# Projection's steps four ahead of the attention's, column sums in the projection's spare bank, and another order of ScalarE's work at a group's turn

## The chip, the cores and the metric

The kernel runs on one core of a Trainium2 chip. The metric is the device time of one execution in microseconds (us); it is given as the median of three runs. Beside it stands one execution taken with the hardware profiler, from which all rows of the profile come. PE is TensorE's matmul row, PEld its weight loads, DVE VectorE, ACT ScalarE, POOL GpSimd and SP SyncE; a small q behind a name means the queue that issues transfers.

## The reference

Four images x of 64 x 64 pixels and 256 channels go through one self-attention layer in float32. Cut to what matters:

```python
q = einsum('bwhc,cd->bwhd', x, Wq) + bq        # d = 128
k = einsum('bwhc,cd->bwhd', x, Wk) + bk
v = einsum('bwhc,cd->bwhd', x, Wv) + bv        # 256 channels
pq, pk, pv = (t.reshape(B, -1, N) for t in (q, k, v))   # N = 4096
energy = einsum('bcn,bcm->bnm', pq, pk)
attention = softmax(energy, axis=-1)
out = einsum('bcm,bnm->bcn', pv, attention)
return gamma * out.reshape(x.shape) + x
```

## The kernel before, in words

**Forms.** A float32 operand is split into a high form h (ScalarE, a scaled copy that is rounded to the matmul's type), a rest l and a combined form d (VectorE, two instructions). A product then is three matmuls instead of one, and each product's accumulator is corrected between two of them.

**Attention.** The loop `for n in range(B * STEPS)` runs 512 steps: 4 images (b) x 8 groups (g) of 512 columns n x 16 steps (t) of 256 rows m. What a step n issues belongs to several steps, since the work is pipelined: the energies of step n + 2 (LOOK = 2), the forms of n + 1, and the attention's product of n. In order: `cross(n + 2)` (two matmuls, L298, into the two banks of `ps_e`, and two scalings by ScalarE, L299), `attend(n, 0)` (six matmuls L355 into the banks a0 and b0), `energy(n + 2)` (four matmuls L313 and two Exp by ScalarE, L316, into x), `upper(n + 2)` (ScalarE's h of it, L322), `halves(n + 1)` (VectorE: L331 adds x to the running column sum s, L336 makes l, L338 makes d), `attend(n, 1)` (six matmuls L355 into a1 and b1). Each engine takes its instructions in the order in which the program issues them; the schedule is written by hand and nothing reorders it. So a step is 18 matmuls of 512 columns on TensorE, and on ScalarE two L299, two L316 and one L322.

**The turn of a group.** a0, a1, b0 and b1 accumulate over the 16 steps of a group. At t = 15, `sum_forms` splits the column sums s into zf (ScalarE L378, VectorE L379, issued ahead of `halves`), and `emptied(n, 0)` copies a0 and b0 into the buffer o (two ScalarE instructions, L369). At t = 0 of the next group, right after `cross`, `emptied(n - 1, 1)` copies a1 and b1, and `sums(n - 1)` multiplies zf by ones (two matmuls, L384) into bank b1 and lets ScalarE copy one row of the result, L385. Then `finish`, a generator that moves on by one piece at the end of each step, takes reciprocals by way of two small DRAM buffers (zd, rd), scales o, adds x by a GpSimd transfer, and stores the result.

**Projection.** Image 0 is projected ahead of the loop. The images 1 to 3 are projected inside it, one image ahead: each of the 16 blocks i of an image takes 8 of the loop's steps, and `step(n, engine)` issues what belongs to r = n mod 8. TensorE has four transposes at r = 0 (L191), the first part of q and k at r = 3 (four matmuls of 256 columns, L222), their second part at r = 4 (eight), the first of v at r = 5 and its second at r = 6. ScalarE has x's h at r = 1 (L202), the h of q and k at 5 (L248), v's bias at 6 (L240) and v's h at 7 (L153). VectorE has one or two instructions at r = 0, 1, 2, 3 (L233, which seeds the second part), 5, 6 and 7. The projection's accumulators rotate over the two banks of the pool `ps_p`. The last image's 128 steps have no projection beside them. Since 16 is twice 8, r = t mod 8: the turn's two steps, t = 15 and t = 0, have r = 7 and r = 0.

**Transfers.** GpSimd's queue stores the forms of q, k and v to DRAM (kf, qd and vf, issued by `store()`, one step after VectorE has made them), loads k for step n + 5 in each step (L285, three buffers), q once a group at t = 6, and in the last group of an image v of the next image, one piece a step from t = 3 on. SyncE's queue loads x for the projection (L183), and carries zd, rd and the output.

Of the kernel before, what the change touches and what calls it, by code (L numbers as in the profile page):

```python
# [9 lines left out]
F32 = mybir.dt.float32  # L10
# [5 lines left out]
PSUM = bass.MemoryType.PSUM  # L16
# [4 lines left out]
def kernel(  # L21
# [37 lines left out]
    B, W, H, C = x.shape  # L59
    P = 128  # L60
# [21 lines left out]
    NB = 512  # L82
    NJ = NB // P
    NG = N // NB
    NU = NM // 2
    STEPS = NG * NU
    LOOK = 2
# [13 lines left out]
    with ExitStack() as fast:  # L101
        fast.enter_context(tc.manual_schedule())
        pool = lambda name, bufs, **kw: fast.enter_context(
            tc.tile_pool(name=name, bufs=bufs, **kw)
        )
# [3 lines left out]
        kpool = pool("kpool", 3)  # L109
        dram = pool("dram", 2, space=DRAM)  # L110
        ps_e = pool("ps_e", 2, space=PSUM)
        ps_p = pool("ps_p", 2, space=PSUM)
        ps_o = pool("ps_o", 1, space=PSUM)


# [27 lines left out]
        qd, kf, vf, units, loads, now = {}, {}, {}, {}, {}, {}  # L143
# [20 lines left out]
        def image(b):  # L164
            for g in range(NG):
                qd[b, g] = dram.tile([P, NJ, 3, P], F32R, tag=f"qd{g}", name=f"qd_{b}_{g}")
            for t in range(NU):
                kf[b, t] = dram.tile([P, 2, 3, P], F32R, tag=f"kf{t}", name=f"kf_{b}_{t}")
                vf[b, t] = dram.tile([P, 3, 2, C], F32R, tag=f"vf{t}", name=f"vf_{b}_{t}")

        def bank(name, shape):
            pool, tag = next(now["banks"])
            return pool.tile(shape, F32, tag=tag, name=name)

        def load_x(b, i):
            if i >= NI:
                return
            if b == 0:
                t = xs4[:, i % 4]
            else:  # L180
                t = work.tile([P, 2, XB], F32, tag="xin", name=f"x_{b}_{i}", bufs=1)
            if b or i:
                nc.sync.dma_start(t, xv[b, i])  # L183
            loads["x", b, i] = t
# [107 lines left out]
        def cross(n):  # L292

            if n >= B * STEPS:
                return
            for i in range(2):
                e = units["e", n, i] = ps_e.tile([P, NB], F32, tag="e", name=f"e_{n}_{i}")
                nc.tensor.matmul(e, *forms(n, i, 2), start=True, stop=False, skip_group_check=True)  # L298
                nc.scalar.mul(e, e, -REST)  # L299
# [18 lines left out]
        def upper(n):  # L318
            if n >= B * STEPS:
                return  # L320
            h = ppool.tile([P, 2, NB], F32R, tag="h", name=f"h_{n}", bufs=3)
            nc.scalar.activation(h, units[n], AF.Identity, scale=UPPER)  # L322
            units[n] = units[n], h
# [40 lines left out]
        def emptied(n, j):  # L364

            if j == 0:
                now["o"] = work.tile([P, 2, 2, NB], F32, tag="o", name=f"o_{n // NU}", bufs=1)
            for c, scale in enumerate((gam2, gam1)):
                nc.scalar.activation(  # L369
                    now["o"][:, c, j, :], now["ab"[c], j], AF.Identity, scale=scale  # L370
                )

        def sum_forms(n):

            s = now["total"] = now["sum"]
            f = work.tile([P, 2, NB], F32R, tag="r", name=f"zf_{n // NU}", bufs=1)
            h, l = now["z"] = f[:, 0, :], f[:, 1, :]
            nc.scalar.activation(h, s[:, 0, :], AF.Identity, scale=UPPER)  # L378
            nc.vector.tensor_tensor(l, s[:, 0, :], h.bitcast(F32), ALU.subtract)  # L379

        def sums(n):
            zp = ps_o.tile([P, NB], F32, tag="b1", name=f"z_{n // NU}")
            for f, x in enumerate(now["z"]):
                nc.tensor.matmul(zp, ones_r, x, start=(f == 0), stop=(f == 1))  # L384
            nc.scalar.copy(now["total"][0:1, 0, :], zp[0:1, :])  # L385
# [35 lines left out]
        def finish_last(n, xr):  # L421

            b, g = B - 1, NG - 1
            attend(n, 0)
            zp = ps_e.tile([P, NJ], F32, tag="e", name="zp")
            for j in range(NJ):
                nc.tensor.matmul(
                    zp[:, j : j + 1], now["sum"][:, 0, j::NJ], ones[:, :1], start=True, stop=True
                )
            r4 = rall[:, B * NG - 1, :]  # L430
            nc.vector.reciprocal(r4, zp)
            work_ = ppool.tile([P, 2, NB], F32, tag="x", name="last")
            spread, ok = work_[:, 0].rearrange("p (q j) -> p q j", j=NJ), work_[:, 1, : B * NG * NJ]
            nc.vector.tensor_tensor(
                spread,
                ident.unsqueeze(2).to_broadcast([P, P, NJ]),
                r4.unsqueeze(1).to_broadcast([P, P, NJ]),
                ALU.mult,
            )
            inside(ok, rall.rearrange("p n j -> p (n j)"))  # L440
            nc.vector.tensor_reduce(zs, ok, AX.X, ALU.min)
            emptied(n, 0)
            o = now["o"]
            attend(n, 1, (2,))
            rp = ps_e.tile([P, NB], F32, tag="e", name="rp")
            nc.tensor.matmul(rp, ones, work_[:, 0], start=True, stop=True)
            attend(n, 1, (0, 1))
            np_ = ps_p.tile([P, 1], F32, tag="p", name="np")
            nc.tensor.matmul(np_, ones, zs, start=True, stop=True)
            nc.scalar.activation(o[:, 1, 1, :], now["b", 1], AF.Identity, scale=gam1)  # L450
            r = work.tile([P, NB], F32, tag="r", name="r_last", bufs=1)
            nc.scalar.copy(r, rp)
            nc.vector.tensor_tensor(o[:, 0, 0, :], o[:, 0, 0, :], o[:, 1, 0, :], ALU.add)
            nc.vector.tensor_tensor(o[:, 0, 0, :], o[:, 0, 0, :], r, ALU.mult)
            nc.vector.tensor_tensor(xr[:, 0, :], xr[:, 0, :], o[:, 0, 0, :], ALU.add)
            nc.sync.dma_start(og[b, g][:, 0], xr[:, 0, :])
            nc.vector.tensor_tensor(o[:, 1, 1, :], o[:, 1, 1, :], r, ALU.mult)
            nc.vector.tensor_tensor(xr[:, 1, :], xr[:, 1, :], o[:, 1, 1, :], ALU.add)
            nc.vector.scalar_tensor_tensor(o[:, 0, 1, :], now["a", 1], gam2, r, ALU.mult, ALU.mult)
            nc.vector.tensor_tensor(xr[:, 1, :], xr[:, 1, :], o[:, 0, 1, :], ALU.add)  # L460
            nc.sync.dma_start(og[b, g][:, 1], xr[:, 1, :])
            nc.vector.tensor_scalar(again, np_, P - 0.5, None, ALU.is_lt)
# [4 lines left out]
        def step(n, engine):  # L467
# [44 lines left out]
                        next(made["v"])  # L512

        now["made"] = {}
        now["banks"] = cycle(
            [(ps_o, "a0"), (ps_o, "a1"), (ps_o, "b0"), (ps_o, "b1"), (ps_p, "p"), (ps_p, "p")]
        )
        image(0)
        for i in range(3):
            load_x(0, i)  # L520
# [6 lines left out]
        for i in range(NI):  # L527
# [35 lines left out]
                load_k(i - 6)  # L563
            if i in (13, 15):
                load_k(i // 2 - 3)
        now["banks"] = cycle([(ps_p, "p")])
        for n in range(B * STEPS):
            b, u = divmod(n, STEPS)
            g, t = divmod(u, NU)
            final = n == B * STEPS - 1  # L570
            if u == 0 and b + 1 < B:
                image(b + 1)
                load_x(b + 1, 0)
            if n == B * STEPS - 6:
                xr = ppool.tile([P, 2, NB], F32, tag="s", name="xr")
                nc.sync.dma_start(xr, xg[b, g])
            cross(n + LOOK)
            if t == 0 and n:
                emptied(n - 1, 1)
            if t == NU - 1 and not final:  # L580
                sum_forms(n)
            step(n, "act")
            if not final:
                attend(n, 0)
            energy(n + LOOK)
            load_k(n + LOOK + 3)
            store()
            if t == 0 and n:
                sums(n - 1)
                active.append(finish(n // NU - 1, now["o"], now["total"]))  # L590
            if t == NU - 1 and not final:
                emptied(n, 0)
            upper(n + LOOK)
            step(n, "pe")
            halves(n + 1)
            step(n, "dve")
            if final:
                finish_last(n, xr)
                break
            attend(n, 1)  # L600
            if t == 6 and n + NU < B * STEPS:
                load_q(*divmod(n // NU + 1, NG))
            if n >= STEPS - NU + 3 and (n - 3) // NU % NG == NG - 1 and (n - 3) // STEPS + 1 < B:
                load_v((n - 3) // STEPS + 1, (n - 3) % NU)
            proceed()

    NB = 512
# [3 lines left out]
    with tc.If(nc.values_load(again[0:1, 0:1]) > 0), ExitStack() as general:  # L611
        pool = lambda name, bufs, **kw: general.enter_context(
            tc.tile_pool(name=name, bufs=bufs, **kw)
        )
# [208 lines left out]
```

## Time and profile before

| | |
|---|---|
| median of three runs | 2421.97 us (2421.1 to 2422.91) |
| the profiled execution's own time | 2424.35 us |
| its span in the profile | 2422.6 us |
| mean granted TensorE clock | 0.994 |
| busy: PE, PEld, DVE, ACT, POOL | 97%, 81%, 88%, 77%, 24% |
| steady attention step without projection work | 4.08 us between two starts of L298 |

A matmul's row lasts longer than the distance to the next one, since matmuls overlap; distances between starts are what counts on PE. In the timeline the columns are the start in us, the time in us that a run of equal instructions covers, the engine, line, operation, out<-in, the count, and in brackets the idle time of the engine ahead of it with what ended it. In the view of waits the columns are the total in us, the number of times, and the longest one.

### The profile page before, as it was taken

What the parts mean: (1) busy time and instruction counts of PE and PEld (TensorE: products, weight loads), DVE (VectorE), ACT (ScalarE), POOL (GpSimd) and SP (SyncE); (2) the same over time, 40 slices, a digit from 0 to 9 for tenths busy, and PEclk for the clock granted to TensorE, in tenths of its full rate; (3) what the DMA queues carried; (4) which work ended last, traced back from release to release, by engine and by line L of the source; (5) the groups of instructions that cost most, each with busy time, mean ns of one, the idle gap of its engine ahead of it and who ended that gap; (6) DMA issues with size and microseconds to landing.
All of it is one profiled execution on the core that took longest, in us unless ns stands there. A gap on an engine that the chain in (4) does not pass through costs nothing.

```text
span 2422.6 us, 31905 instructions
## 1 busy us (share of the span) xinstructions
PE 2358.6 (97%) x11094; PEld 1954.4 (81%) x11094; DVE 2138.0 (88%) x2126; ACT 1870.8 (77%) x3076; POOL 581.7 (24%) x943
## 2 busy tenths in 40 slices
PE   6799999999999999999999999999999999999998
PEld 6688888888888888888888888888888888888886
DVE  7789988889989899888899898898888888888887
ACT  4577777877877877778778778778777778787875
POOL 5422222222322222212233122222123111111110
PEclk9999999999999999999999999999999999999999
DMA  9756655656796666566699566675569644444443
GB/s 200 169 143 166 180 143 158 177 156 181 217 296 171 168 164 181 146 158 178 157 284 265 147 165 166 170 181 147 154 176 315 198 127 131 120 119 125 120 123 92
DMA packets 243990, 413.82 MB, mean 171 GB/s; under 512 B 26031, under 2 KB 141487, under 8 KB 243822
## 3 DMA queue, kind: packets, MB, share of 16 engines
q0 software_dynamic: 203152, 368.77, 57.2%
q1 hardware_dynamic: 40126, 42.67, 6.4%
q8 instruction: 91, 1.49, 0.3%
q14 instruction: 77, 0.63, 0.1%
q10 hardware_dynamic: 544, 0.26, 0.0%
HBM read 306.64 MB, written 104.98 MB: 170 GB/s over the span
## 4 chain that ended last, share of the span: by engine, by line
PE 86%; ACT 9%; DMA 2%; DVE 1%; issue 1%; POOL 0%; SPq 0%; DVEq 0%; ACTq 0%
PE a L355 35%; PE b L355 17%; PE e L313 17%; PE e L298 9%; PE qv L222 7%; ACT o L369 3%; ACT e L299 2%; ACT x L316 1%; ACT h L322 1%; PE z L384 1%; PE xt L191 1%; DMA k<-kf 1%; DMA qd<-f 1%; ACT zf L378 1%; DVE v L156 0%
## 5 line engine op out<-in xcount | busy, mean ns | idle before, releaser
L316 ACT ACTIVATE x<-e 128x512 f32<-128x512 f32 x960 | 523.8, 600 | 319.1 <-PE e L313 316.0
L285 POOL DMA_DIRECT2D k<-kf x512 | 275.8, 539 | 1743.3 <-PE e L313 1638.6
L331 DVE TENSOR_TENSOR s<-s,x 128x1024 f32<-128x1024 f32 x480 | 585.8, 1220 | 95.1 <-ACT x L316 92.7
L299 ACT ACTIVATE e<-e 128x512 f32<-128x512 f32 x1024 | 547.4, 574 | 137.2 <-PE e L298 136.5
L355 PE MATMUL a<-h,v 128*128 128x512 f32 x2048 | 640.0, 394 | 0.0
L355 PE MATMUL a<-ld,v 128*128 128x512 f32 x2048 | 633.4, 390 | 0.0
L355 PE MATMUL b<-ld,v 128*128 128x512 f32 x2048 | 631.7, 390 | 0.0
L336 DVE TENSOR_TENSOR ld<-x,h 128x1024 fp32r<-128x1024 f32 x480 | 585.4, 1220 | 30.9 <-PE b L355 24.8
L338 DVE SCALAR_TENSOR_TENSOR ld<-h,x 128x1024 fp32r<-128x1024 f32 x480 | 584.4, 1218 | 0.0
L313 PE MATMUL e<-q,k 128*128 128x512 f32 x2048 | 552.0, 391 | 4.5
L322 ACT ACTIVATE h<-x 128x1024 fp32r<-128x1024 f32 x480 | 509.9, 1062 | 13.3
L313 PEld LDWEIGHTS e<-q,k 128*128 128x128 f32 x2048 | 379.4, 188 | 98.1 <-ACT e L299 23.2
L355 PEld LDWEIGHTS a<-ld,v 128*128 128x128 f32 x2048 | 385.1, 188 | 83.2
L355 PEld LDWEIGHTS b<-ld,v 128*128 128x128 f32 x2048 | 383.9, 188 | 82.8 <-ACT s L385 1.4
L355 PEld LDWEIGHTS a<-h,v 128*128 128x128 f32 x2048 | 369.3, 189 | 62.7 <-issue 1.0
L298 PE MATMUL e<-q,k 128*128 128x512 f32 x1024 | 316.3, 390 | 0.6 <-DMA k<-kf 0.6
L298 PEld LDWEIGHTS e<-q,k 128*128 128x128 f32 x1024 | 192.0, 188 | 42.3 <-issue 1.6
L222 PE MATMUL qv<-wf,xf 128*128 128x256 f32 x768 | 117.6, 290 | 26.0 <-DVE qv L233 25.9
L222 PEld LDWEIGHTS qv<-wf,xf 128*128 128x128 f32 x768 | 109.1, 194 | 37.4 <-DVE qv L233 29.5
L222 PEld LDWEIGHTS qv<-xf,wf 128*128 128x128 f32 x768 | 108.8, 193 | 7.5
L222 PE MATMUL qv<-xf,wf 128*128 128x256 f32 x768 | 113.9, 285 | 0.0
L270 POOL DMA_DIRECT2D kf<-f x128 | 98.4, 769 | 41.0 <-ACT xf L202 20.6
(79 smaller groups left out, 1215.1 us busy)
## 6 DMA issues: line engine op xcount, KB each, us to landing
k<-kf POOLq DMA_DIRECT2D x512, 384.0 KB, 3.5
vf<-vf POOLq DMA_DIRECT2D x48, 768.0 KB, 6.0
v<-vf POOLq DMA_DIRECT2D x48, 768.0 KB, 7.2
kf<-f POOLq DMA_DIRECT2D x128, 192.0 KB, 3.4
qd<-f POOLq DMA_DIRECT2D x128, 192.0 KB, 3.1
q<-qd POOLq DMA_DIRECT2D x32, 768.0 KB, 4.7
o<-in_x_dram POOLq DMA_DIRECT2D x31, 512.0 KB, 7.7
out_dram<-o SPq DMA_DIRECT2D x31, 512.0 KB
```

Source lines behind the costliest of these rows:

```text
L222: nc.tensor.matmul(to[:, s, :], left, right.rearrange("p s a -> p (s a)") if w else right, start=(f == 2 and s == k == 0), stop=(f == 1 an ...
L270: nc.gpsimd.dma_start(to, f)
L285: nc.gpsimd.dma_start(t, kf[b, u % NU])
L298: nc.tensor.matmul(e, *forms(n, i, 2), start=True, stop=False, skip_group_check=True)
L299: nc.scalar.mul(e, e, -REST)
L313: nc.tensor.matmul(e, *forms(n, i, f), start=False, stop=(f == 1), skip_group_check=True)
L316: nc.scalar.activation(x[:, i, :], e, AF.Exp, scale=(1.0 + E) ** 3 / E)
L322: nc.scalar.activation(h, units[n], AF.Identity, scale=UPPER)
L331: nc.vector.tensor_tensor(s, s, x, ALU.add)
L336: nc.vector.tensor_tensor(l, x, h.bitcast(F32), ALU.subtract)
L338: nc.vector.scalar_tensor_tensor(d, h.bitcast(F32), 1.0 + E, x, ALU.mult, ALU.subtract)
L355: nc.tensor.matmul(to, vall[:, t, f, i, j * P : (j + 1) * P], units[n][f][:, i, :], start=(t == 0 and i == 0 and f != 1), stop=(t == NU - ...
```

## The change

The pool `ps_p` has two tags of one bank each instead of one tag with two; a counter `now["turn"]` picks the bank, and `spare` returns the bank that the projection will take next without moving the counter. `sums` takes that bank instead of b1. `sum_forms` becomes a generator of two pieces. In the loop `step(p, ...)` gets p = n up to n = 7, two values of p in each of the steps 8 to 11 (the second one after `attend(n, 1)`), and p = n + 4 from n = 12 on. The image's DRAM tiles and its first x are fetched at u = 123 of the image before instead of u = 0. At the turn the order of calls differs; the others stand as they were.

```diff
-        ps_p = pool("ps_p", 2, space=PSUM)
+        ps_p = pool("ps_p", 1, space=PSUM)
...
         def bank(name, shape):
-            pool, tag = next(now["banks"])
+            tile_ = spare(name, shape)
+            now["turn"] += 1
+            return tile_
+
+        def spare(name, shape):
+            pool, tag = now["banks"][now["turn"] % len(now["banks"])]
             return pool.tile(shape, F32, tag=tag, name=name)
...
             nc.scalar.activation(h, s[:, 0, :], AF.Identity, scale=UPPER)
+            yield
             nc.vector.tensor_tensor(l, s[:, 0, :], h.bitcast(F32), ALU.subtract)
+            yield
 
         def sums(n):
-            zp = ps_o.tile([P, NB], F32, tag="b1", name=f"z_{n // NU}")
+            zp = spare(f"z_{n // NU}", [P, NB])
...
-        now["banks"] = cycle([(ps_p, "p")])
+        now["turn"], now["banks"] = 0, now["banks"][4:]
         for n in range(B * STEPS):
...
-            if u == 0 and b + 1 < B:
-                image(b + 1)
-                load_x(b + 1, 0)
+            if n == 0:
+                image(1)
+                load_x(1, 0)
+            if u == STEPS - 5 and b + 2 < B:
+                image(b + 2)
+                load_x(b + 2, 0)
...
             cross(n + LOOK)
+            turn = t == NU - 1 and not final
             if t == 0 and n:
-                emptied(n - 1, 1)
-            if t == NU - 1 and not final:
-                sum_forms(n)
-            step(n, "act")
+                upper(n + LOOK - 1)
+            if turn:
+                zf = sum_forms(n)
+                next(zf)
+            p = n if n < 8 else 2 * n - 8 if n < 12 else n + 4
+            step(p, "act")
             if not final:
                 attend(n, 0)
             energy(n + LOOK)
             load_k(n + LOOK + 3)
             store()
             if t == 0 and n:
+                emptied(n - 1, 1)
+            if turn:
+                emptied(n, 0)
+            else:
+                upper(n + LOOK)
+            step(p, "pe")
+            if t == 0 and n:
                 sums(n - 1)
                 active.append(finish(n // NU - 1, now["o"], now["total"]))
-            if t == NU - 1 and not final:
-                emptied(n, 0)
-            upper(n + LOOK)
-            step(n, "pe")
             halves(n + 1)
-            step(n, "dve")
+            if turn:
+                next(zf)
+            step(p, "dve")
             if final:
                 finish_last(n, xr)
                 break
             attend(n, 1)
+            if 8 <= n < 12:
+                for engine in ("act", "pe", "dve"):
+                    step(p + 1, engine)
```

So ScalarE's order over the two steps of a turn (t = 15, then t = 0) goes

- before: L299 x2, L378, L153, L316 x2, L369 x2 (a0, b0), L322 | L299 x2, L369 x2 (a1, b1), L316 x2, L385, L322
- after: L299 x2, L378, L316 x2, L369 x2 (a0, b0) | L299 x2, L322, L316 x2, L369 x2 (a1, b1), L322, L385

by the line numbers of before. On TensorE the sums' two matmuls stand behind the projection's matmuls of that step instead of ahead of them. As p = n + 4, the turn's two steps have r = 3 and r = 4 in place of r = 7 and r = 0. The stores of a block's q and k go from t = 7 and 15 to t = 3 and 11, those of v from t = 9 and 1 to t = 5 and 13, the loads of x from t = 1 and 9 to t = 5 and 13.

More of the change, by code (lines that the diff above doesn't have):

```diff
@@ L447, in finish_last @@
             attend(n, 1, (0, 1))
-            np_ = ps_p.tile([P, 1], F32, tag="p", name="np")
+            np_ = ps_p.tile([P, 1], F32, tag="p0", name="np")
             nc.tensor.matmul(np_, ones, zs, start=True, stop=True)
@@ L514 @@
         now["made"] = {}
-        now["banks"] = cycle(
-            [(ps_o, "a0"), (ps_o, "a1"), (ps_o, "b0"), (ps_o, "b1"), (ps_p, "p"), (ps_p, "p")]
-        )
+        now["turn"], now["banks"] = 0, [(ps_o, tag) for tag in ("a0", "a1", "b0", "b1")]
+        now["banks"] += [(ps_p, "p0"), (ps_p, "p1")]
         image(0)
```

## The prediction

> **What bounds the kernel now.** I read the page's busy shares first, then the view of waits, then the timeline of one turn, because a share is a mean over stages.
>
> ```profile
> span 2422.6 us, 31905 instructions
> PE 2358.6 (97%) x11094; PEld 1954.4 (81%) x11094; DVE 2138.0 (88%) x2126; ACT 1870.8 (77%) x3076; POOL 581.7 (24%) x943
> ```
>
> ```profile
> PEld z L384 <- ACT o L369: 27.5, 31, 0.9
> PE qv L222 <- DVE qv L233: 25.9, 15, 4.5
> ...
> PEld e L313 <- ACT e L299: 23.2, 62, 0.6
> ...
> PE z L384 <- ACT o L369: 14.0, 31, 0.5
> ...
> PE e L298 <- DMA k<-kf: 0.6, 2, 0.3
> ```
>
> TensorE is the bound. Inside the attention loop it waits at one place that comes back: at each of the 31 turns the sums' matmuls L384 wait for ScalarE's L369, and the energies L313 for its L299. L222's 15 waits lie in the projection of image 0 ahead of the loop (one for each block but one), and L298's two are worth little. What the turn costs is read from starts: TensorE in the turn from 613 us, and after it an ordinary step with the same transposes, r = 0.
>
> ```profile
> 613.01 0.61 PE L298 MATMUL e<-q,k 128*128 128x512 f32 x2
> ...
> 617.09 0.61 PE L298 MATMUL e<-q,k 128*128 128x512 f32 x2
> ...
> 619.21 1.21 PE L313 MATMUL e<-q,k 128*128 128x512 f32 x4
> ...
> 620.88 0.74 PE L384 MATMUL z<-zf,ones 128*128 128x512 f32 x2 [0.45 <-ACT o L369]
> ...
> 621.45 0.60 PE L191 MATMUL xt<-ident,x 128*128 128x128 f32 x4
> ...
> 623.29 0.63 PE L298 MATMUL e<-q,k 128*128 128x512 f32 x2
> ```
>
> ```profile
> 654.83 0.62 PE L298 MATMUL e<-q,k 128*128 128x512 f32 x2
> ...
> 659.38 0.62 PE L298 MATMUL e<-q,k 128*128 128x512 f32 x2
> ```
>
> The 18 matmuls of the step t = 15 take 617.09 - 613.01 = 4.08 us, 0.227 each. The step t = 0 takes 6.20; the ordinary one with transposes 4.55; the two sums' matmuls are worth 2 x 0.227 = 0.45. So 6.20 - 4.55 - 0.45 = 1.20 us of the turn is waiting. It shows in the rows: after 617.09 eight matmuls are due before L313, at 618.91, and it starts at 619.21; four more and z is due at 620.12, but starts at 620.88; and its pair holds 0.57, not 0.45, since the weights of a matmul that waited are not loaded ahead.
>
> Why ScalarE is late:
>
> ```profile
> 613.44 1.07 ACT L299 ACTIVATE e<-e 128x512 f32<-128x512 f32 x2 [0.84 <-PE e L298]
> 614.41 0.63 ACT L378 ACTIVATE zf<-s 128x512 fp32r<-128x512 f32 x1
> 614.93 0.60 ACT L153 ACTIVATE vf<-qv 128x512 fp32r<-128x512 f32 x1
> 615.48 1.09 ACT L316 ACTIVATE x<-e 128x512 f32<-128x512 f32 x2
> 616.45 0.70 ACT L369 ACTIVATE o<-a,gam 128x512 f32<-128x512 f32 x1
> 617.02 0.70 ACT L369 ACTIVATE o<-b,gam 128x512 f32<-128x512 f32 x1
> 617.59 1.08 ACT L322 ACTIVATE h<-x 128x1024 fp32r<-128x1024 f32 x1
> 618.54 1.10 ACT L299 ACTIVATE e<-e 128x512 f32<-128x512 f32 x2
> ...
> 620.10 0.73 ACT L369 ACTIVATE o<-b,gam 128x512 f32<-128x512 f32 x1
> 620.67 1.14 ACT L316 ACTIVATE x<-e 128x512 f32<-128x512 f32 x2
> ...
> 625.13 1.07 PE L313 MATMUL e<-q,k 128*128 128x512 f32 x4
> ...
> 625.78 1.09 ACT L316 ACTIVATE x<-e 128x512 f32<-128x512 f32 x2 [0.48 <-PE e L313]
> ```
>
> From 613.44 to 620.83 it has no gap. From start to start the rows give 0.97 for a pair of L299 or L316, 0.52 for L378, 0.55 for L153, 0.57 for one L369, 0.95 for L322. The L299 that could start 0.43 after its matmul (613.01 to 613.44), at 617.52, starts at 618.54, and the second L369 ends at 620.83, 0.05 before z. Where ScalarE is in time, an Exp comes 0.65 after the first L313 (625.13 to 625.78).
>
> The Trainium skill, "Trainium Kernel Development and Optimization", section Performance Expectations, calls matmul busy time a bad metric because matmuls are pipelined, and the weight loads' share a good one. By PE's idle time at z the turns could give 14.0; by the weight loads' idle time 27.5 + 23.2 = 50.7. The starts give 31 x 1.20 = 37: the trace agrees with the rule that the first is too small, and has the second too large, part of it being the loads' lead. By the one the kernel could end at 2408.0 at best, by the other at 2371.3; to the latter I give no chance, since the starts have no more than 37 to give.
>
> **The change, part by part.** Three edits act together at the turn, so I lay its two steps out again with the durations above. Time 0 is the L298 of t = 15.
>
> The turn's steps now carry r = 3 and r = 4. What these cost on TensorE:
>
> ```profile
> 631.47 0.62 PE L298 MATMUL e<-q,k 128*128 128x512 f32 x2
> ...
> 636.05 0.62 PE L298 MATMUL e<-q,k 128*128 128x512 f32 x2
> ...
> 638.77 1.12 PE L222 MATMUL qv<-wf,xf 128*128 128x256 f32 x8
> ...
> 641.11 0.62 PE L298 MATMUL e<-q,k 128*128 128x512 f32 x2
> ```
>
> r = 3 makes a step 4.58, r = 4 makes it 5.06, so 0.98 for the eight matmuls. TensorE without waits: L298 of t = 0 at 4.58, `attend(n, 0)` at 5.03, L313 at 6.39, L222 at 7.30, z at 8.28, `attend(n, 1)` at 8.73.
>
> ScalarE: L299 at 0.43, L378 at 1.40 (L153 has moved to another step), the Exps 0.65 after their L313 of 1.82, so at 2.47, L369 of a0 at 3.44 and b0 at 4.01, free at 4.58. L299 of t = 0 at 5.01, when its matmul is done: L313 at 6.39 no longer waits for it. L322 at 5.98, free at 6.93; Exps at 6.39 + 0.65 = 7.04; L369 of a1 at 8.01, done 0.70 later, seen by TensorE 0.05 later: 8.76. `attend(n, 1)` wants a1 at 8.73. So the wait doesn't vanish, it goes to a1, and projection's 0.98 covers it: 0.03 and the 0.12 of weights not loaded ahead, 0.15 in all. b1 is wanted 0.91 after a1 and freed 0.57 after it. z itself needs zf's rest: VectorE makes it after l and d of n; z stands at 8.28, and L378 ends at 2.03, so with three VectorE instructions of at most 1.22 (two of them done while it waits) it is there by 6. Its bank held the transposes, read at r = 2. Gain: 1.20 - 0.15 = 1.05 for each turn with projection. p = n + 4 stays below 384, the end of image 3's projection, up to n = 379, so these are 23 of the 31 (n = 16 to 368): 24.2 us.
>
> In the last image there is no projection to cover a1.
>
> ```profile
> 2074.02 0.61 PE L298 MATMUL e<-q,k 128*128 128x512 f32 x2
> ...
> 2077.80 0.73 PE L384 MATMUL z<-zf,ones 128*128 128x512 f32 x2 [0.45 <-ACT o L369]
> ...
> 2079.77 0.62 PE L298 MATMUL e<-q,k 128*128 128x512 f32 x2
> ```
>
> Before: 5.75 - 4.08 - 0.45 = 1.22 of waiting. After, without 0.50 and 0.98: `attend(n, 1)` due at 7.25; ScalarE's L299 at 4.58, L322 at 5.55, Exps at 5.89 + 0.65 = 6.54, a1 at 7.51, seen at 8.26: 1.01 + 0.12 = 1.13 of waiting. Gain 0.09, times 8: 0.7 us.
>
> VectorE at the turn: s + x of n + 1 can go on, l of n + 1 now waits for L322 at 5.98 to 7.04 and d ends 2.4 later, by 9.5; `attend(n + 1, 0)` wants l at 10.26 + 0.91 = 11.2. Queued behind are L331 to L338 of n + 2, wanted a step later. Taken at nothing; without that cover each us late would be paid 31 times.
>
> The second part of q and k (L222) needs VectorE's seed. At r = 3 to 4 of an ordinary step:
>
> ```profile
> 634.87 0.70 DVE L233 SCALAR_TENSOR_TENSOR qv<-qv,bias 128x512 f32<-128x512 f32 x1 [0.39 <-PE qv L222]
> ```
>
> It ends at 635.57, and L222 wants it at 638.77: 3.2 us of cover. At the turn it now stands behind L379 (0.69), which is inside that cover.
>
> Steps 8 to 11 carry two projection steps each, once. TensorE's work is the same, 4 x 4.08 and 0.47 + 0.50 + 0.98 and as much again for v, 19.7 in all. VectorE's:
>
> ```profile
> 622.56 1.21 DVE L331 TENSOR_TENSOR s<-s,x 128x1024 f32<-128x1024 f32 x1
> 623.69 1.21 DVE L336 TENSOR_TENSOR ld<-x,h 128x1024 fp32r<-128x1024 f32 x1
> ```
>
> Three instructions at 1.13 from start to start and at most two of 0.70 are 4.8 a step, 19.2 in all: just under. Bounds: each of the four steps meets a wait for a seed like those of the prologue, 25.9 / 15 = 1.73, so 6.9 us lost, or nothing is lost; a gain is excluded, as TensorE's work there stays the same. I take nothing: the cover of 3.2 in the loop is the nearer row.
>
> Moved transfers: two stores each of kf and qd at t = 3 and 11, one of vf at 5 and 13, so in an image's last group the ones of t = 15 and 1 come inside the stretch in which v is loaded (from t = 3), while those of t = 7 and 9 leave its middle. On SyncE x's load passes ahead of r's at t = 5 and behind the output at t = 13; nothing is due within a step of either. GpSimd's loads of k stand behind the same stores as before, four steps earlier. k is late twice, at image edges, and one of them is:
>
> ```profile
> 672.15 0.63 PE L298 MATMUL e<-q,k 128*128 128x512 f32 x2
> ...
> 677.76 0.70 PE L298 MATMUL e<-q,k 128*128 128x512 f32 x2 [0.35 <-DMA k<-kf]
> ```
>
> The step has r = 4 and takes 5.61 for 5.06: 0.55. Bounds: both waits go (+1.1), or all three edges get two (-2.2). I take +0.5, one of them, because the stores leave the stretch's crowded middle.
>
> **Sum.** 24.2 + 0.7 + 0.5 = 25.4 us off 2424.35, the profiled execution's own time, which is 1.8 more than its span: 2399.0. That execution lies 2.4 above the median of the runs, 2421.97, so 2396.6 there; I say 2397.
>
> **The rivals.**
> - *The wait moves whole to a1* in all turns, as in the last image. For it: a1 still stands behind two Exps. Against: L222's 0.98 lies between. Gain 31 x 0.09 = 2.8: 2419.2, within 0.2% of no change, which is about what a measurement of this kernel can tell.
> - *Half of it stays.* For it: ScalarE's rows grow under load (L369 0.70 to 0.73, L316's pair 1.09 to 1.14), and 0.5 more at a1 would go straight to TensorE. 23 x 0.55 + 0.7 + 0.5 = 13.9: 2408.1. Against: the cover ends 0.03 from even, and nothing in the rows is 0.5 slower.
> - *Slower: the turn's L222 waits for VectorE's seed*, which now stands behind L379, itself behind l and d and waiting for ScalarE. At the prologue's 1.73 each, 23 times, 39.8 lost against 25.4 won: 2436.4. It decides from a seed over 3.2 + 25.4 / 23 = 4.3 us late; against it speaks that VectorE was idle for 3.29 there:
>
> ```profile
> 615.07 0.69 DVE L379 TENSOR_TENSOR zf<-s,zf 128x512 fp32r<-128x512 f32 x1 [3.29 <-ACT zf L378]
> ```
>
> - *More is won*: a1 comes in time everywhere with projection and both waits for k go: 23 x 1.20 + 0.7 + 1.1 = 29.4: 2392.6.
>
> **How the numbers follow.** The forecast has 0.70, with a range of its own from 2392 to 2402. Half stays: 0.14; whole: 0.05; slower by the seed or by something like it: 0.06; more: 0.05. From 2391 to 2410 lie the forecast, what is won more down to no wait at all, and most of the half: 0.8 and a little. Faster by over 0.2% (under 2417): 0.70 + 0.14 + 0.05, and a little of the second rival, 0.90; within: 0.04; slower: 0.06.
>
> **What would show it.** In the changed kernel's profile: no wait of PE at z nor at L313 for L299; a short one of the a product of `attend` for L369, about 0.1 in turns with projection and near 1.0 in the last image's eight; a step t = 0 of about 5.7 in both kinds; VectorE's 3.29 before L379 gone; L222 without waits outside the prologue. A wait for L369 of 0.5 or more in the projecting images, or any for L233 in the loop, would make the prediction wrong, as would more waits for k at the image edges.

## The result, and the profile after

The changed kernel takes 2396.98 us (median of four runs, 2396.34 to 2398.81); the kernel before, on the same chip, 2421.53 us. The ratio is 0.9901, with a 95% interval from 0.9889 to 0.9913: one per cent faster. The forecast was 2397 us.

Below stand the first two lines of the changed kernel's page, then TensorE's whole list of waits and, from the weight loads' list, the line that answers to those of before (total us, times, longest us). The new lines L303, L304, L318, L321, L327, L360, L374, L391 and L392 are the L298, L299, L313, L316, L322, L355, L369, L384 and L385 of before; L227 and L238 are its L222 and L233, and L341, L383 and L385 are its L336, L378 and L379:

```profile
span 2396.9 us, 31876 instructions
PE 2347.5 (98%) x11094; PEld 1961.0 (82%) x11094; DVE 2144.2 (89%) x2126; ACT 1874.7 (78%) x3076; POOL 580.4 (24%) x943
```

```profile
PE qv L227 <- DVE qv L238: 24.8, 15, 4.5
PE a L360 <- ACT o L374: 6.6, 8, 0.8
PE xt L196 <- DMA xs<-in_x_dram: 5.7, 1, 5.7
PE wp L132 <- DVE ones L128: 1.1, 1, 1.1
PE rp L453 <- DVE last L441: 0.4, 1, 0.4
...
PEld a L360 <- ACT o L374: 17.5, 31, 1.3
```

z no longer waits, L318 doesn't either, and the waits for k are gone. In their place stands the wait for a1: the weight loads' row has it at all 31 turns, the matmuls' row only at 8, those of the last image. This is the turn of the same group, TensorE and ScalarE in the timeline of the changed kernel; its t = 15 starts at 607.18:

```profile
611.76 0.61 PE L303 MATMUL e<-q,k 128*128 128x512 f32 x2
...
613.15 1.06 ACT L327 ACTIVATE h<-x 128x1024 fp32r<-128x1024 f32 x1
613.57 1.07 PE L318 MATMUL e<-q,k 128*128 128x512 f32 x4
614.22 1.09 ACT L321 ACTIVATE x<-e 128x512 f32<-128x512 f32 x2
...
614.48 1.11 PE L227 MATMUL qv<-wf,xf 128*128 128x256 f32 x8
615.20 0.69 ACT L374 ACTIVATE o<-a,gam 128x512 f32<-128x512 f32 x1
...
615.43 0.63 PE L391 MATMUL z<-zf,ones 128*128 128x512 f32 x2
...
615.94 0.73 PE L360 MATMUL a<-h,v 128*128 128x512 f32 x2
...
617.44 0.62 PE L303 MATMUL e<-q,k 128*128 128x512 f32 x2
```

With 607.18 taken off these are 4.58 for t = 0, 5.97 for L327, 7.04 for the Exps, 8.02 for a1's copy, 8.25 for z and 8.76 for `attend(n, 1)`. The prediction had 4.58, 5.98, 7.04, 8.01, 8.28 and 8.76. The step takes 617.44 - 611.76 = 5.68, of which 5.06 are matmuls of an ordinary step with r = 4 and 0.45 the sums: 0.17 of waiting. In the last image:

```profile
2049.40 0.62 PE L303 MATMUL e<-q,k 128*128 128x512 f32 x2
...
2052.84 0.69 ACT L374 ACTIVATE o<-a,gam 128x512 f32<-128x512 f32 x1
...
2053.58 0.73 PE L360 MATMUL a<-h,v 128*128 128x512 f32 x2 [0.82 <-ACT o L374]
...
2055.08 0.39 PE L303 MATMUL e<-q,k 128*128 128x512 f32 x1
```

Here the step is 5.68 too, but 4.08 and 0.45 of it are work and 1.15 is waiting, against 1.22 before.

### The profile page after: what moved, and what is told of

Its sections match the earlier page's. It is cut to its first block, busy times and chain, and to the rows that moved or that the text cites. A ratio compares the mean times of both kernels' runs of the same rounds, so it can differ in the third digit from the quotient of the medians.

```text
span 2396.9 us, 31876 instructions
## 1 busy us (share of the span) xinstructions
PE 2347.5 (98%) x11094; PEld 1961.0 (82%) x11094; DVE 2144.2 (89%) x2126; ACT 1874.7 (78%) x3076; POOL 580.4 (24%) x943
## 4 chain that ended last, share of the span: by engine, by line
PE 94%; ACT 2%; DVE 1%; DMA 1%; issue 0%; POOL 0%; SPq 0%; DVEq 0%; ACTq 0%
PE a L360 39%; PE b L360 19%; PE e L318 19%; PE e L303 10%; PE qv L227 7%; PE xt L196 1%; ACT x L321 1%; ACT o L374 1%; DMA qd<-f 1%; DVE v L156 0%; PE z L391 0%; DVE f L256 0%; DMA xs<-in_x_dram 0%; DVE qv L238 0%; ACT h L327 0%; ACT e L304 0%
## 5 line engine op out<-in xcount | busy, mean ns | idle before, releaser
L321 ACT ACTIVATE x<-e 128x512 f32<-128x512 f32 x960 | 521.9, 596 | 298.5 <-PE e L318 292.1
L336 DVE TENSOR_TENSOR s<-s,x 128x1024 f32<-128x1024 f32 x480 | 586.8, 1222 | 104.0 <-ACT x L321 101.9
L341 DVE TENSOR_TENSOR ld<-x,h 128x1024 fp32r<-128x1024 f32 x480 | 586.3, 1222 | 86.5 <-ACT h L327 55.8
L360 PE MATMUL a<-h,v 128*128 128x512 f32 x2048 | 643.5, 395 | 6.6 <-ACT o L374 6.6
L360 PE MATMUL a<-ld,v 128*128 128x512 f32 x2048 | 633.3, 390 | 0.0
L304 ACT ACTIVATE e<-e 128x512 f32<-128x512 f32 x1024 | 546.4, 572 | 109.7 <-PE e L303 109.0
L360 PE MATMUL b<-ld,v 128*128 128x512 f32 x2048 | 631.5, 390 | 0.0
L318 PE MATMUL e<-q,k 128*128 128x512 f32 x2048 | 547.6, 389 | 0.0
L327 ACT ACTIVATE h<-x 128x1024 fp32r<-128x1024 f32 x480 | 510.5, 1063 | 13.6
L360 PEld LDWEIGHTS a<-ld,v 128*128 128x128 f32 x2048 | 385.0, 188 | 83.6
L360 PEld LDWEIGHTS b<-ld,v 128*128 128x128 f32 x2048 | 384.3, 188 | 82.1
L318 PEld LDWEIGHTS e<-q,k 128*128 128x128 f32 x2048 | 384.3, 188 | 79.7
L360 PEld LDWEIGHTS a<-h,v 128*128 128x128 f32 x2048 | 368.5, 189 | 80.0 <-ACT o L374 17.5
L303 PE MATMUL e<-q,k 128*128 128x512 f32 x1024 | 316.4, 390 | 0.0
L303 PEld LDWEIGHTS e<-q,k 128*128 128x128 f32 x1024 | 192.1, 188 | 40.6
L227 PE MATMUL qv<-wf,xf 128*128 128x256 f32 x768 | 117.7, 290 | 24.9 <-DVE qv L238 24.8
L227 PEld LDWEIGHTS qv<-wf,xf 128*128 128x128 f32 x768 | 109.1, 194 | 36.3 <-DVE qv L238 28.3
L227 PEld LDWEIGHTS qv<-xf,wf 128*128 128x128 f32 x768 | 109.4, 195 | 7.5
L227 PE MATMUL qv<-xf,wf 128*128 128x256 f32 x768 | 114.5, 286 | 0.0
```

The source lines that it names most:

```text
L227: nc.tensor.matmul(to[:, s, :], left, right.rearrange("p s a -> p (s a)") if w else right, start=(f == 2 and s == k == 0), stop=(f == 1 an ...
L318: nc.tensor.matmul(e, *forms(n, i, f), start=False, stop=(f == 1), skip_group_check=True)
L321: nc.scalar.activation(x[:, i, :], e, AF.Exp, scale=(1.0 + E) ** 3 / E)
L336: nc.vector.tensor_tensor(s, s, x, ALU.add)
L341: nc.vector.tensor_tensor(l, x, h.bitcast(F32), ALU.subtract)
L360: nc.tensor.matmul(to, vall[:, t, f, i, j * P : (j + 1) * P], units[n][f][:, i, :], start=(t == 0 and i == 0 and f != 1), stop=(t == NU - ...
```

## The experiments

Each kernel was timed against the kernel before on the same chip; ratios are to it.

**The lead alone.** From the kernel before:

```diff
-            step(n, "act")
+            p = n if n < 8 else 2 * n - 8 if n < 12 else n + 4
+            step(p, "act")
...
             attend(n, 1)
+            if 8 <= n < 12:
+                for engine in ("act", "pe", "dve"):
+                    step(p + 1, engine)
```

with the fetch of x as in the changed kernel.

> The kernel before with the lead alone (p = n + 4, two steps of projection in each of the loop's steps 8 to 11, x fetched five steps before the image's end); the sums stay in bank b1 and ahead of projection's matmuls, ScalarE's order stays. Theory (the three edits share the gain): L153 has left the turn, so with time 0 at the L298 of t = 15 ScalarE's L369 of b1 ends at 7.79 and z, due at 7.30, comes at 7.84: 0.54 and 0.12 of weights not loaded ahead, 0.66 of waiting instead of 1.20 in the 23 turns with projection, unchanged in the last image's 8. Gain 12.4, and about 1 for the two waits for k: 2408, ratio 0.994 to 0.995. Rival 1 (the lead does it all): 2397, 0.990. Rival 2 (the lead is only a prerequisite for the bank and wins nothing): 2421, 1.000.

Measured: 2409.23 us, ratio 0.9953 (0.9936 to 0.9969). Its timeline at a turn:

```profile
607.70 0.62 PE L298 MATMUL e<-q,k 128*128 128x512 f32 x2
...
612.28 0.62 PE L298 MATMUL e<-q,k 128*128 128x512 f32 x2
...
614.79 0.72 ACT L369 ACTIVATE o<-b,gam 128x512 f32<-128x512 f32 x1
...
615.56 0.72 PE L384 MATMUL z<-zf,ones 128*128 128x512 f32 x2 [0.34 <-ACT o L369]
...
618.46 0.62 PE L298 MATMUL e<-q,k 128*128 128x512 f32 x2
```

6.18 - 5.06 - 0.45 = 0.67 of waiting at z, as the theory had it, and the waits for k are gone in this kernel too. The lead gives about half of the gain, and both rivals fall.

The theory's reason for it does not hold, though. L153's leaving made nothing come earlier: counted from the L298 of t = 15, ScalarE's copy of b1 ends 7.81 us later here (614.79 + 0.72 - 607.70) and 7.82 later in the kernel before (620.10 + 0.73 - 613.01). The Exps start 2.47 after that L298 in both, so before L153 filled a gap ahead of them. What the lead changed is TensorE's side: t = 15 now has the four matmuls of r = 3 and takes 4.58 instead of 4.08, so z is wanted half a microsecond later, and that is the half microsecond of waiting saved.

Why the waits for k went is not settled. The stretch in which the next image's v is loaded (t = 3 of an image's last group to t = 2 of the next) holds as many stores as before, at other steps, and the loads of x have moved too. What the traces show is that the longest load of k in the first such stretch took 11.0 us from issue to landing before and 7.9 here.

**The sums back in b1.** From the changed kernel:

```diff
-            zp = spare(f"z_{n // NU}", [P, NB])
+            zp = ps_o.tile([P, NB], F32, tag="b1", name=f"z_{n // NU}")
```

> The changed kernel with the sums back in bank b1 and all else kept. Theory: z then waits for the L369 of b1, which the new order has put behind two Exps: in a turn with projection due at 8.28, free at 9.33 (time 0 at the L298 of t = 15), 1.17 of waiting against 0.15; in the last image due at 6.80, free at 8.83, 2.15 against 1.13. So 31 x 1.02 = 32 lost: 2429, ratio 1.003, slower than before. Rival (the bank doesn't matter, since the a product behind z waits for the same two instructions anyway): 2397 to 2400, 0.990 to 0.991.

Measured: 2432.28 us, ratio 1.0048 (1.0032 to 1.0065): slower than before. At a turn of the last image:

```profile
2074.80 0.62 PE L303 MATMUL e<-q,k 128*128 128x512 f32 x2
...
2079.56 0.72 PE L391 MATMUL z<-zf,ones 128*128 128x512 f32 x2 [1.88 <-ACT o L374]
...
2081.53 0.63 PE L303 MATMUL e<-q,k 128*128 128x512 f32 x2
```

6.73 - 4.08 - 0.45 = 2.20 of waiting where 2.15 was expected. So the new order of ScalarE is only bearable with the sums in another bank: b1 is emptied last in it.

Two of the last image's eight turns took longer, 8.24 and 8.19 us in place of 6.73, after the same wait. This is the first of them, with its row of the view by stretches, in which the last three numbers are the granted clock, the DMA share and GB/s:

```profile
2005.29 0.62 PE L303 MATMUL e<-q,k 128*128 128x512 f32 x2
...
2010.05 1.13 PE L391 MATMUL z<-zf,ones 128*128 128x512 f32 x2 [1.88 <-ACT o L374]
...
2013.53 0.66 PE L303 MATMUL e<-q,k 128*128 128x512 f32 x2
```

```profile
2010.05:2013.53 3.48, 3.48 (x8) 2.71 (x9) 1.34 (x2) 1.47 (x2) 0.00 (x0) 0.52 0.28 94
```

The granted clock was 0.52 there, against 1.00 in the stretch from 110 to 2000 us. The two turns and the steps after them lost 3.2 us in this profiled execution, whose loop is 35.6 us longer than the changed kernel's where the theory had 32.

**ScalarE's order of before, with the lead and the bank.** From the changed kernel:

```diff
             if t == 0 and n:
-                upper(n + LOOK - 1)
+                emptied(n - 1, 1)
...
-            if t == 0 and n:
-                emptied(n - 1, 1)
             if turn:
                 emptied(n, 0)
-            else:
-                upper(n + LOOK)
+            upper(n + LOOK)
```

> The changed kernel with ScalarE's order of before at the turn (L322 of n + 1 at t = 15, L369 of a1 and b1 right after the L299 pair of t = 0); lead, bank and VectorE's order kept. Theory (the new order is not needed once the bank and the lead are there, and costs what is left at a1): with time 0 at the L298 of t = 15, L322 at 4.58, L299 at 5.53, so L313 at 6.39 finds it done; a1 free at 7.25, wanted at 8.73: no wait in the 23 turns with projection, 0.15 each saved. In the last image L313 is due at 5.89 and L299 seen at 6.16: 0.39 of waiting against 1.13. Together 23 x 0.15 + 8 x 0.74 = 9.4 saved: 2388, ratio 0.986. Rival (the new order brings a good part of the gain): the wait of L313 for L299 comes back in all turns, 0.3 to 0.4 each, 2400 to 2408, 0.991 to 0.994.

Measured: 2389.17 us, ratio 0.9871 (0.9855 to 0.9888), its interval below the changed kernel's. A turn of the last image:

```profile
2042.41 0.62 PE L303 MATMUL e<-q,k 128*128 128x512 f32 x2
2042.91 1.08 ACT L327 ACTIVATE h<-x 128x1024 fp32r<-128x1024 f32 x1
2043.86 1.09 ACT L304 ACTIVATE e<-e 128x512 f32<-128x512 f32 x2
2044.52 0.30 PEld L318 LDWEIGHTS e<-q,k 128*128 128x128 f32 x2 [0.56 <-ACT e L304]
...
2047.41 0.62 PE L303 MATMUL e<-q,k 128*128 128x512 f32 x2
...
2051.60 0.39 PE L303 MATMUL e<-q,k 128*128 128x512 f32 x1
```

5.00 - 4.53 = 0.47 of waiting at t = 0, and 0.11 more at t = 1 (4.19 for 4.08), together 0.58 against the changed kernel's 1.15. In the turns with projection a step t = 0 takes 5.54 to 5.58 there, 5.56 in the mean, not 5.68. The new order thus costs 0.12 in 23 turns and 0.57 in 8, 2.8 + 4.6 = 7.4 of the 7.8 us that the two medians are apart. Of the change's three parts the order is the one that takes away.

From the lead alone to this kernel two things change that bear on z, the bank of the sums and their place behind the projection's matmuls, and in the turns with projection no run parts them. (VectorE's order changes too; a run further down shows that it is worth nothing.) The copy of b1 ends there 7.81 us after the L303 of t = 15, ahead of z's 8.28, so for that copy alone z could have stayed in b1; but L392, which reads z, ends at 10.34, and b's product is wanted at 9.64 (8.73 + 0.91 in the prediction). In the last image, where TensorE has no projection, the place makes no difference, and there the step t = 0 went from 5.75 to 5.00 (and t = 1 from 4.09 to 4.19).

**A lead of two.** From the changed kernel, so that the turn's steps have r = 1 and 2:

```diff
-            if u == STEPS - 5 and b + 2 < B:
+            if u == STEPS - 3 and b + 2 < B:
...
-            p = n if n < 8 else 2 * n - 8 if n < 12 else n + 4
+            p = n if n < 8 else 2 * n - 8 if n < 10 else n + 2
...
-            if 8 <= n < 12:
+            if 8 <= n < 10:
```

> The changed kernel with a lead of two steps instead of four (p = n + 2, two steps of projection in the loop's steps 8 and 9): the turn's steps have r = 1 and r = 2, in which TensorE has nothing of projection; the same work in all, other steps longer. Theory (projection's 0.98 us of matmuls cover the wait for a1): every turn waits as in the last image, 1.13 instead of 0.15 in 23 turns, 22.5 lost: 2419.5, ratio 0.999. Rival (the gain is the bank's and the order's alone, wherever projection stands): 2397, 0.990.

Measured: 2418.22 us, ratio 0.9990 (0.9980 to 0.9999). The list of TensorE's waits has one line for it, now at all 31 turns:

```profile
PE a L360 <- ACT o L374: 25.5, 31, 0.8
```

The turn with projection now waits as the last image's does, so it is TensorE's eight matmuls at r = 4 that hide the wait for a1, and with ScalarE's new order the gain hangs on which r falls on t = 0.

**VectorE's order of before.** From the changed kernel, zf's rest ahead of `halves`:

```diff
-            halves(n + 1)
             if turn:
                 next(zf)
+            halves(n + 1)
```

> The changed kernel with VectorE's order of before at the turn: zf's rest (L379) ahead of l and d of n, so VectorE waits there for ScalarE's L378 again. Theory (VectorE's order wins nothing here: its idle time of 97 us in 31 turns is not on the path): L379 then runs from 2.1 to 2.8 (time 0 at the L298 of t = 15), l and d end by 5.1, wanted by the b product at 5.9; the seed ends by 5.7, wanted at 7.3: no wait on TensorE, 2397, ratio 0.990. Rival (the idle time of VectorE was part of what was won): a wait of TensorE for VectorE's l, d or seed at the turn, 0.2 us or more each, so 2403 or more, 0.9925 or more.

Measured: 2395.89 us, ratio 0.9896 (0.9881 to 0.9911), the changed kernel's. VectorE's list of waits in this run has

```profile
DVE zf L385 <- ACT zf L383: 66.0, 31, 2.6
```

while TensorE has the same waits for ScalarE as in the changed kernel. In the changed kernel VectorE's idle time stands elsewhere, at l, which waits for L327: 74.9 us in all there, 8.5 here, so 66.0 + 8.5 = 74.5. The order moves this idle time and does not end it, and in either place some 2 us at each turn cost TensorE nothing.

**The copies around L327.** From the changed kernel, `emptied` taking the banks to copy:

```diff
             if t == 0 and n:
+                emptied(n - 1, 1, (0,))
                 upper(n + LOOK - 1)
+                emptied(n - 1, 1, (1,))
...
-            if t == 0 and n:
-                emptied(n - 1, 1)
```

> The changed kernel with a third order of ScalarE's work at t = 0: L299 pair, L369 of a1, L322 of n + 1, L369 of b1, Exps, L322 of n + 2, L385. Theory (the turn waits for whatever ScalarE does late, and each instruction has its own time at which it is wanted): in turns with projection a1 is free at 6.7 for 8.73, b1 at 8.3 for 9.64, L313 finds L299 done: at most 0.05 of waiting instead of 0.15. In the last image a1 free at 6.3 for 7.25, b1 at 7.8 for 8.16, L313 without wait; what is left is L385, which puts the L299 of the next step at 10.05, seen at 10.68 by an L313 that is due at 10.42: about 0.45 of waiting in t = 0 and 1 together instead of 1.13. So 23 x 0.1 + 8 x 0.7 = 8 saved against the changed kernel: 2389, ratio 0.9865. Rival (ScalarE is simply too full at the turn, any order leaves the same): 2395 to 2397, 0.989 to 0.990.

Measured: 2387.48 us, ratio 0.9863 (0.9848 to 0.9878). In the last image:

```profile
2041.60 0.62 PE L303 MATMUL e<-q,k 128*128 128x512 f32 x2
...
2046.20 0.66 PE L303 MATMUL e<-q,k 128*128 128x512 f32 x2
...
2047.30 0.56 ACT L392 COPY s<-z 1x512 f32<-1x512 f32 x1
2047.77 1.04 ACT L304 ACTIVATE e<-e 128x512 f32<-128x512 f32 x2
2048.39 0.30 PEld L318 LDWEIGHTS e<-q,k 128*128 128x128 f32 x2 [0.60 <-ACT e L304]
```

t = 0 takes 4.60, 0.07 over its work; what is left is at t = 1, where L392, the copy of the sums' row, stands ahead of an L304 that L318 waits for (4.61 for 4.08 up to the next L303, at 2050.81). Together that is 0.60 where 0.45 was expected, and no less than the 0.58 of the order of before. In the turns with projection t = 0 takes 5.50, with no waiting left, so the rival falls.

**And the row's copy later.** From the kernel of the run just shown, L392 behind the L304 pair of t = 1, where `finish` starts; `sums` keeps its result in `now["zp"]` and no longer copies the row:

```diff
             cross(n + LOOK)
+            if t == 1 and n > 1:
+                nc.scalar.copy(now["total"][0:1, 0, :], now["zp"][0:1, :])
+                active.append(finish(n // NU - 1, now["o"], now["total"]))
...
                 sums(n - 1)
-                active.append(finish(n // NU - 1, now["o"], now["total"]))
...
             nc.sync.dma_start(row(zd), s[0:1, 0, :])
-            yield
             nc.sync.dma_start(r4, spread(zd))
```

> As the run with the copies around L322, and L385 (the copy of the sums' row) goes behind the L299 pair of t = 1; finish starts there, with its first two transfers in one piece. Theory: L299 of t = 1 is done before its L313 in the last image too, so at most 0.15 of waiting is left at a turn in either kind: 8 x 0.3 saved against the run without it: 2386 to 2387, ratio 0.9855. Rival: the row comes later to the reciprocal, VectorE waits for it at t = 3 and TensorE behind it: 2389 or more, 0.9865 or more.

Measured: 2383.52 us, ratio 0.9846 (0.9833 to 0.9860), the fastest of all. A turn of the last image:

```profile
2040.31 0.62 PE L303 MATMUL e<-q,k 128*128 128x512 f32 x2
...
2044.91 0.66 PE L303 MATMUL e<-q,k 128*128 128x512 f32 x2
...
2049.07 0.62 PE L303 MATMUL e<-q,k 128*128 128x512 f32 x2
```

Two steps in 8.76, of which 8.61 are work (2 x 4.08 and 0.45): 0.15 of waiting, as expected. VectorE's list has no wait for the row in the loop, so the rival falls. The row's copy was not moved with ScalarE's order of before.

The bank alone, without the lead, was not tried, nor, with ScalarE's order of before, the sums in their later place but in b1. With r = 0 at t = 0 the bank that comes next still holds v's accumulator, which VectorE reads only later in that step.

## Why the prediction was right, point by point

- *TensorE is the bound, and it waits at the turn.* Right, and read from starts the size was right too: 37 us of waiting at 31 turns. With the fastest kernel's last order nearly all of it is gone: 2421 to 2384, of which about 1 us belongs to the waits for k.
- *The laid-out turn with projection.* Right to 0.03 at each instruction shown above. 0.17 of waiting came for 0.15, with 0.02 more at t = 1 (617.44 to 622.04 is 4.60, for 4.58), and the usual turn of before waited 1.18, not the 1.20 of the one that was shown. So a turn gained about 1.0 for 1.05, 23 us for 24.2.
- *The last image.* Right: t = 0 took 5.68 against 5.75 before, 0.6 us over the eight turns where 0.7 was forecast.
- *The waits for k.* The direction was right, the size too small: both went, 1.2 us for 0.5 (0.55 and 0.44 in the two steps, and 0.1 in the step after each). The run with the lead alone shows that the lead did it; that it was the stores' leaving the crowded middle, as the prediction has it, is not shown.
- *Steps 8 to 11.* Right: the starts of L303 give 4.56, 4.58, 5.56 and 5.09 for the four steps, of which 0.03 in step 11 is over its work.
- *VectorE at the turn, the seed, the moved order of L379.* Right that all of it lies beside other work: TensorE's list has no wait for VectorE inside the loop (the 15 at L227 lie ahead of it, as before), and the run with VectorE's order of before has the same time. VectorE's wait ahead of L379 is gone, but most of it came back at l.
- *The sum.* 23 + 0.6 + 1.2 = 24.8 is what the parts give; between the starts of steps 1 and 508 the two traces are 24.6 apart. The two spans are 25.6 apart. Of the rest 0.3 is in the loop's first step (5.79 before, 5.47 after), 0.1 ahead of it and 0.6 behind the start of step 508. The first step differs in the granted clock, 0.77 before and 0.82 after, and it takes 5.16 to 5.54 in the experiments; these outer parts differ from run to run. The forecast of 25.4 was made of slightly too much at the turns and too little at k.

What it did not do is cost the three edits one by one; it laid out their joint effect and called them one. The runs part them but for one place: the lead alone is 11.9 us faster than before, the lead with the bank and the sums' later place 31.9, all three 24.6. The prediction laid out L153 as gone from the turn; its going won nothing there, and the lead's own part is the matmuls of r = 3 and r = 4, which let TensorE want z and, in the changed kernel, a1 later. So the wait at a1, which the prediction found and priced, was not the price of moving z, but of ScalarE's new order, and with the order of before there is none at a1, only 0.05 in a turn with projection and the 0.58 us at L318 in the last image's turns.

The rivals: the wait that moves whole to a1 is what the lead of two shows, 2418.2 us for the 2419.2 that was worked out; in the changed kernel r = 4 prevents it. Half of it did not stay: a1's copy came 0.01 later than laid out, not 0.5, and 0.17 of waiting is left. Slower by the seed never came near, as TensorE never waited for VectorE in the loop. Of the last rival, that more is won, one half came true: both waits for k went, but a1 still waited. The Trainium skill, "Trainium Kernel Development and Optimization", section Performance Expectations, calls matmul busy time a bad metric for how close a kernel is to roofline, and the weight loads' busy share a good one. The first half is borne out here: matmul idle time alone was 14.0 us and starts gave 37, of which some 36 could be had. The second holds only as a hint, since the weight loads' idle time was 50.7.

## What to carry to other kernels

Where an engine is the bound, read what it loses from the distances between the starts of one instruction, stage by stage, not from its idle time. Then lay out the neighbour's instructions with the time at which each result is wanted. The order that serves the earliest want first beat the rearrangement that only moved the wait (2387.5 against 2397.0 us). Against the order that stood there before (2389.2) it was clearly ahead only once the row's copy had moved too (2383.5). Cost each edit of a bundle alone as well, and check the reason along with the number: here one of three edits gave back a quarter of what the others won, and the gain of another came from the waiting engine's later want, not from the work taken off the engine that it waited for.

## What the runs showed of the hardware that was not expected

The loop repeats to 0.01 or 0.02 us from turn to turn and between kernels (steps of 4.08, 4.58 and 5.06 in all of them), with few exceptions. So a schedule laid out by hand from a dozen rows held to 0.03 us over the changed kernel's two steps and to 3.5 us over a whole kernel, in seven further kernels; the worst miss at a turn is the 0.58 for 0.39 in the last image with ScalarE's order of before, leaving aside the two turns told of next.

The largest exception is the granted clock. In the run with the sums back in b1 TensorE stood idle for 1.88 us in each of the last image's eight turns. In two of them the granted clock was then 0.52 and 0.53 over the rest of the step, and the step took 8.24 and 8.19 us instead of 6.73; in the other six it did not. The other kernels, whose waits at a turn were 0.82 us or less, show 1.00 from 106 to 2365 us. So a longer wait can cost a second time, though what decides in which turns it does was not tested.

Outside the loop's steady part the profiled executions differ ahead of the loop, in its first step (5.16 to 5.79 us) and behind its last steps.
